# Values of an attention layer from seven products of halves, with output projections and a graph layer's values at other places

## The chip, the cores and the metric

The kernel runs on one core of one Trainium2 chip. The metric is device time in microseconds (us) of one execution. The core has TensorE (PE, matmuls; its weight loads are shown apart as PEld), VectorE (DVE), ScalarE (ACT), GpSimd (POOL) and SyncE (SP, which issues most DMAs here). [...]

## The reference, cut to what matters

Input is x (32, 512, 512) in float32: 32 batches of 512 nodes with 512 features. Two layers follow each other, each with a residual and a layer norm:

```python
x = _layernorm(x + _L0_gnn_ref(x, adj, W, a))     # graph attention: h = x @ W, softmax over e, alpha @ h
x = _layernorm(x + _L1_gnn_ref(x, adj, ...))      # 8 heads of 64, masked by adj

q, k, v = (split_heads(h @ W.T + b) for W, b in ((Wq, bq), (Wk, bk), (Wv, bv)))
scores = where(adj == 0, -inf, q @ k.T / 8)
out = softmax(scores) @ v                          # then out @ Wo.T + bo
```

The change concerns h @ Wv.T (the values, a 512x512x512 product per batch), and where out @ Wo.T and layer 0's alpha @ h stand in the order of work.

## The kernel before, in words

**Tiling.** Everything is float32. A batch is four tiles of 128 nodes. [...] Of the eight banks four (`ps_s`) are for attention scores; four (`ps_m`) go round for all else, the one that was given back first being taken first.

**Stretches.** The main loop takes, for each batch b, four pairs of heads (hp = 0 to 3). One turn is called a stretch here. In each stretch TensorE makes the scores of node tiles 0 and 1 (`head_scores`, ps, L593), then some other work (the first filler), then the scores of tiles 2 and 3, then probabilities times values of the pair before (`head_values`, pav, L628), then more other work (the second filler). The fillers are the rest of the model: layer 0 of the next batches (ph, po), the q and k projection of the next two pairs of heads (`project_two`, pw, L503), the values (`project_v`, pv, L575 calling L249) and the output projection of the batch before (`finish`, pf, L649).

**What the other engines do in a stretch.** VectorE subtracts the maximum from each of eight score tiles (L297), ScalarE takes the exponential (L602), VectorE transposes the eight results in blocks of 32 (L312) into a tile t, and takes the reciprocal of the row sums (tot, L611). SyncE then writes the sums out (d_tot, L613) and issues sixteen DMAs that move t into pt (L329), which `head_values` of the next stretch reads. There is one t, one pt and one tile for the inverted sums (inv, L616, two DMAs on POOL's queue), so each waits for the readers of the one before. After `head_values`, VectorE scales its result into ot (L636).

**Layer 0, one batch ahead.** In stretch hp 3, behind pt's sixteen issues, SyncE has three more DMAs in this order: d_most (512 single numbers to DRAM, L395), x of the next batch but one (1 MB, L145) and row (a read of d_most to all partitions, L400, which waits for the landing of d_most). In the next hp 0 stretch VectorE subtracts row from the scores (`l0_weights`, et, L429) and POOL adds h to x (`l0_add_h`, L355), when they have landed. In hp 1 `l0_values` (po, L437) follows, and the layer norm.

**Seven products.** `project_two` multiplies with seven products of half-sized blocks and sums of blocks instead of eight. The sums of weights are made once (`weight_sums`, L226), the sums of layer 1's input per batch (tx, `x1_sums`, L482 to L485, on POOL). A product is four matmuls of 256 columns; intermediate results are copied out by ScalarE (L527), one is added to another by POOL (p7, L555), and VectorE adds them to the last products (L539). The values use no such scheme: four tiles, each four matmuls of 512 columns and a copy on ScalarE (L576).

**What sets the order.** PE, DVE, ACT and SP keep the order in which the program calls the functions. POOL's order is chosen by a scheduler.

Of the kernel before, what the change touches and what calls it, by code (L numbers as in the profile page):

```python
# [14 lines left out]
P = 128  # L15
# [11 lines left out]
def kernel(  # L27
# [53 lines left out]
    PB = 9  # L81
# [34 lines left out]
    wqx_sb = const.tile([P, 3, 2, 2, P], F32, name="wqx_sb")  # L116
    wkx_sb = const.tile([P, 3, 2, 2, P], F32, name="wkx_sb")
    wv_sb = const.tile([P, FC, F], F32, name="wv_sb")
    wo_sb = const.tile([P, FC, F], F32, name="wo_sb")
    bq_sb = const.tile([P, FC], F32, name="bq_sb")  # L120
    bqs_sb = const.tile([P, FC], F32, name="bqs_sb")
# [21 lines left out]
    def load_x(b):  # L143
        x_sb = io.tile([P, NB, F], F32, name=f"x_{b}", tag="x", bufs=3)
        nc.sync.dma_start(x_sb, x[b].rearrange("(c p) f -> p c f", p=P))  # L145
        st["x1", b] = x_sb
# [79 lines left out]
    def weight_sums():  # L226

        for c in range(FC):  # L230
            nc.scalar.activation(wq_sb[:, c, :], wq_sb[:, c, :], AF.Identity, scale=SCALE)
        for w_t, x_t in ((wq_sb, wqx_sb), (wk_sb, wkx_sb)):
            v = w_t.rearrange("p c (s i d) -> p c s i d", s=2, i=2)
            lo, hi = slice(0, FC // 2), slice(FC // 2, FC)
            a11, a21 = v[:, lo, :, 0], v[:, lo, :, 1]
            a12, a22 = v[:, hi, :, 0], v[:, hi, :, 1]
            s1, s2, s4 = (x_t[:, i] for i in range(3))
            nc.vector.tensor_tensor(s1, a21, a22, ALU.add)
            nc.scalar.activation(a22, a22, AF.Identity, scale=-1.0)
            nc.vector.tensor_tensor(s2, s1, a11, ALU.subtract)  # L240
            yield
            nc.vector.tensor_tensor(s4, a12, s2, ALU.subtract)
            nc.vector.tensor_tensor(a21, a11, a21, ALU.subtract)
            yield

    def matmul_f(ps, lhs, rhs):

        for c in range(FC):
            nc.tensor.matmul(ps, lhs(c), rhs(c), start=(c == 0), stop=(c == FC - 1))  # L249

    def psum(name):
        return ps_m.tile([P, N], F32, name=name, tag="m")
# [139 lines left out]
    def l0_write(b):  # L392
        d = dram.tile([N], F32, name=f"d_most_{b}", tag="dmost")
        with nc.allow_non_contiguous_dma(reason="512 numbers"):
            nc.sync.dma_start(d.rearrange("(i p) -> p i", p=P), st["most", b])  # L395
        st["most", b] = d

    def l0_read(b):
        row = prob.tile([P, N], F32, name=f"row_{b}", tag="row", bufs=1)
        nc.sync.dma_start(row, st["most", b].partition_broadcast(P))  # L400
        st["row", b] = row
# [30 lines left out]
    def l0_values(b, i):  # L432
        h_sb, z = st["h", b], st["x1", b]
        et = st["et", b]
        po = ps_m.tile([P, F1 + 1], F32, name=f"po_{b}_{i}", tag="m")
        for j in range(NB):
            nc.tensor.matmul(  # L437
                po,
                et[:, j, i * P : (i + 1) * P],
                h_sb[:, j, 2:],  # L440
                start=(j == 0),
                stop=(j == NB - 1),
            )
        inv = small.tile([P, 1], F32, name=f"inv0_{b}_{i}", tag="inv0", bufs=2)
        nc.vector.reciprocal(inv, po[:, F1:])
        nc.vector.scalar_tensor_tensor(
            z[:, i, :F1], po[:, :F1], inv, z[:, i, :F1], ALU.mult, ALU.add
        )
# [119 lines left out]
        yield  # L568
        result(1, 0, b4, u2)

    def project_v(b, i):
        x1t = st["x1t", b]
        v = act.tile([P, F], F32, name=f"v_{b}_{i}", tag="v", bufs=6)
        ps = psum(f"pv_{b}_{i}")
        matmul_f(ps, lambda c: x1t[:, i, c, :], lambda c: wv_sb[:, c, :])  # L575
        nc.scalar.copy(v, ps)  # L576
        st["v", b, i] = v

    def head_scores(b, hp, i):
        qk = st["qk", b, hp]  # L580
# [41 lines left out]
    def head_values(b, hp, bank=None):  # L622
        pt, inv = st.pop(("pt", b, hp)), st.pop(("inv", b, hp))
        po = (bank or psum)(f"pav_{b}_{hp}")
        for c in range(NB):
            for j in range(2):
                head = 2 * hp + j
                nc.tensor.matmul(  # L628
                    po[j * D : (j + 1) * D, :],
                    st["v", b, c][:, head * D : (head + 1) * D],  # L630
                    pt[:, :, j, c, :, :].rearrange("p g i q -> p g (i q)"),
                    start=(c == 0),
                    stop=(c == NB - 1),
                )
        ot = act.tile([P, N], F32, name=f"ot_{b}_{hp}", tag="ot", bufs=6)
        nc.vector.tensor_tensor(  # L636
            ot.rearrange("p (g i q) -> p g i q", g=4, i=NB),
            po.rearrange("p (g i q) -> p g i q", g=4, i=NB),
            inv.rearrange("p (g q) i -> p g i q", g=4),
            ALU.mult,  # L640
        )
        st["ot", b, hp] = ot
# [37 lines left out]
    def steps(todo):  # L680
        for _ in todo:
            pass
# [18 lines left out]
        if i > 0:  # L701
            l0_norm(0, [i - 1])
    l0_norm(0, [NB - 1])
    steps(sums)
    masks1()
    l0_project(1, 0)
    l0_project(1, 1)
# [2 lines left out]
    l0_project(1, 3)  # L710
    l0_columns(1)
    x1_sums(0, nc.vector)
    project_v(0, 0)
    project_v(0, 1)
    steps(project_two(0, 0))
    l0_maxima(1)
    l0_write(1)
    l0_read(1)
    before = None
    for b in range(B):  # L720
        more = b < B - 1
        for hp in range(NP):

            head_scores(b, hp, 0)
            head_scores(b, hp, 1)
            if hp == 0:
                if more:
                    l0_scores(b + 1)  # L730
                if b > 1:
                    project_v(b, 0)
                if b > 0 and more:
                    project_v(b, 1)
            elif hp == 1:
                if more:
                    for i in range(NB):
                        l0_values(b + 1, i)
                        if i < NB - 1:
                            ln_stats(st["x1", b + 1], f"0_{b + 1}", i)  # L740
                else:
                    finish(b - 1, 0)
                if b + 2 < B:
                    load_xt(b + 2)
            elif hp == 2:
                if b > 0 and more:
                    finish(b - 1, 0)
                if b > 0 and more:
                    add_bias(b + 1)
            else:  # L750
                if b > 0:
                    if not more:
                        finish(b - 1, 3)
                    store(b - 1)
                if b + 2 < B:
                    for i in range(NB):
                        l0_project(b + 2, i)
                    l0_columns(b + 2)
                if b == 0:
                    project_v(1, 0)  # L760
            head_scores(b, hp, 2)
            head_scores(b, hp, 3)
            head_blocks(b, hp)
            if before is not None:
                head_values(*before)
            if hp == 3 and b + 2 < B:
                l0_maxima(b + 2)
                l0_write(b + 2)
                load_x(b + 2)
                l0_read(b + 2)  # L770
            if hp == 0:
                if not more:
                    project_v(b, 1)
                project_v(b, 2)
                project_v(b, 3)
                if more:
                    l0_weights(b + 1)
                    l0_add_h(b + 1)
            elif hp == 1:
                two = project_two(b, 1)  # L780
                if more:
                    ln_stats(st["x1", b + 1], f"0_{b + 1}", NB - 1)
                    ln_root(f"0_{b + 1}")
                if more:
                    l0_norm(b + 1)
                steps(two)
                if more:
                    x1_blocks(b + 1)
                    x1_sums(b + 1, nc.gpsimd)
            elif hp == 2:  # L790
                if b == 0:

                    pb = psum("pb")
                    matmul_f(
                        pb,
                        lambda c: bv_sb[:, c : c + 1].to_broadcast([P, P]),
                        lambda c: wo_sb[:, c, :],
                    )
                    nc.vector.tensor_tensor(bo_sb, pb, bo_sb, ALU.add)
                    add_bias(0)  # L800
                    add_bias(1)
                else:
                    finish(b - 1, 1)
                    finish(b - 1, 2)
                if b > 0 and more:
                    finish(b - 1, 3)
            elif more:
                steps(project_two(b + 1, 0))
            before = (b, hp)
    b = B - 1  # L810
# [64 lines left out]
```

## Time and profile before

| | |
|---|---|
| median of 3 runs | 3187.83 us (3183.2 to 3192.03) |
| the profiled execution | 3189.21 us, its span 3187.4 us |
| TensorE busy | 3131.1 us (98%) |
| VectorE, ScalarE, POOL busy | 2462.6, 1398.4, 772.8 us (77%, 44%, 24%) |
| SyncE's DMA queue | 434.23 MB, 56.9% of sixteen engines |
| mean granted TensorE clock | 0.994 |

The profile page counts busy time per engine, idle time with what ended it, and the chain of work that ended last. A float32 matmul stands as two instructions in it. The timeline gives start and length of merged instructions in us from the span's start, and in brackets the idle time before them and what ended it. In the text T0 is the start of a batch's hp 0 stretch on TensorE, T1 to T3 of the others.

### The profile page before, as it was taken

Reading aid. Unit: us, or ns where it says so; the run is one execution under the profiler, and the core shown is the slowest. Engines: PE = TensorE matmul, PEld = TensorE weight load, DVE = VectorE, ACT = ScalarE, POOL = GpSimd, SP = SyncE. Lnnn points to the kernel's source line nnn. Section 1 sums busy time; section 2 is a strip of 40 time slices with the busy share of each in tenths; the row PEclk is TensorE's granted clock in tenths of the full one; section 3 lists DMA queues with packets and bytes.
Section 4 is the critical chain, followed back from the end, with each engine's and each line's share of the span. In section 5 each row is a group of like instructions: output and inputs, shape, how many; then the busy total and the mean of one; then the engine's idle time right before and its main releaser. Section 6 shows DMA issues by size and latency. Waiting matters only on the chain.

```text
span 3187.4 us, 40275 instructions
## 1 busy us (share of the span) xinstructions
PE 3131.1 (98%) x11844; PEld 1769.4 (56%) x11844; DVE 2462.6 (77%) x5665; ACT 1398.4 (44%) x3057; POOL 772.8 (24%) x869
## 2 busy tenths in 40 slices
PE   7999999999999999999999999999999999999997
PEld 5555556555555555565565565555555555655543
DVE  4777777787778877787877787877788777878766
ACT  2444444444444444444444444444444444344432
POOL 1222221222222222312222222222223222222210
PEclk9999999999999999999999999999999999999999
DMA  5566566666666655665666565666666665656654
GB/s 155 126 156 149 148 146 159 138 148 154 153 141 155 154 146 148 148 160 143 149 159 148 144 156 142 151 151 154 144 153 152 151 147 139 162 136 152 137 136 116
DMA packets 259819, 470.64 MB, mean 148 GB/s; under 512 B 107472, under 2 KB 110032, under 8 KB 259600
## 3 DMA queue, kind: packets, MB, share of 16 engines
q1 hardware_dynamic: 247136, 434.23, 56.9%
q0 software_dynamic: 12464, 33.84, 4.1%
q8 instruction: 95, 1.56, 0.2%
q14 instruction: 124, 1.02, 0.1%
HBM read 132.65 MB, written 34.27 MB: 52 GB/s over the span
## 4 chain that ended last, share of the span: by engine, by line
PE 93%; DMA 3%; DVE 1%; issue 1%; SPq 1%; ACT 0%; DVEq 0%; ACTq 0%
PE pw L503 24%; PE ps L593 14%; PE pav L628 14%; PE pf L649 14%; PE pv L249 13%; PE po L437 7%; PE ph L249 7%; DMA d_most<-most 2%; SPq L329 1%; DMA pt<-t 0%; DMA row<-d_most 0%; DVE t L312 0%; DVE p L297 0%; DMA rows<-d_att 0%; DVE junk L297 0%
## 5 line engine op out<-in xcount | busy, mean ns | idle before, releaser
L602 ACT ACTIVATE p<-p,least 128x512 f32<-128x512 f32 x1024 | 725.5, 710 | 751.0 <-issue 402.4
L297 DVE CUSTOM_DVE_ANT_0 p<-ps,mask 128x512 f32<-128x512 f32 x1024 | 643.1, 684 | 296.4 <-PE ps L593 296.2
L312 DVE STREAM_TRANSPOSE t<-p 128x512 f32<-128x512 f32 x1024 | 622.4, 675 | 1.7 <-ACT p L602 1.5
L593 PE MATMUL ps<-qk 64*128 64x512 f32 x2048 | 513.5, 617 | 5.1 <-DVE least L297 4.9
L628 PE MATMUL pav<-pt,v 128*64 128x512 f32 x2048 | 469.8, 601 | 10.1 <-DMA pt<-t 4.4
L649 PE MATMUL pf<-wo_sb,ot 128*128 128x512 f32 x1024 | 459.7, 602 | 4.9 <-DVE ot L636 4.9
L249 PE MATMUL pv<-wv_sb,x1t 128*128 128x512 f32 x1024 | 456.6, 598 | 0.0
L616 POOL DMA_DIRECT2D inv<-d_tot x256 | 134.4, 528 | 1073.1 <-DVE least L297 560.0
L649 PEld LDWEIGHTS pf<-wo_sb,ot 128*128 128x128 f32 x1024 | 190.0, 191 | 271.8 <-issue 263.6
L249 PEld LDWEIGHTS pv<-wv_sb,x1t 128*128 128x128 f32 x1024 | 189.3, 190 | 263.7 <-issue 256.7
L593 PEld LDWEIGHTS ps<-qk 64*128 64x128 f32 x2048 | 178.5, 186 | 269.1 <-issue 187.8
L628 PEld LDWEIGHTS pav<-pt,v 128*64 128x64 f32 x2048 | 137.4, 137 | 327.8 <-issue 274.5
L437 PE MATMUL po<-h,et 128*128 128x257 f32 x1024 | 236.0, 389 | 6.8 <-ACT et L430 4.9
L249 PE MATMUL ph<-w_sb,xt 128*128 128x258 f32 x1024 | 235.8, 388 | 3.2 <-ACT x1t L468 2.9
L437 PEld LDWEIGHTS po<-h,et 128*128 128x128 f32 x1024 | 194.6, 193 | 59.2 <-ACT et L430 26.4
L249 PEld LDWEIGHTS ph<-w_sb,xt 128*128 128x128 f32 x1024 | 194.1, 192 | 54.9 <-DVE mv L263 22.0
L418 POOL TENSOR_TENSOR et<-et,mask0t 128x512 f32<-128x512 f32 x126 | 142.1, 1157 | 317.6 <-ACT et L414 317.6
L492 POOL TENSOR_TENSOR x<-x,bo_sb 128x512 f32<-128x512 f32 x128 | 158.4, 1271 | 190.6 <-DVE x1t_b L312 170.7
L602 ACT ACTIVATION_READ_ACCUMULATOR p<-p,least 128x1 f32 x1024 | 191.4, 187 | 0.0
L262 DVE BATCH_NORM_STATS2 stats<-x 128x6 f32<-128x512 f32 x256 | 177.6, 694 | 13.9
L576 ACT COPY v<-pv 128x512 f32<-128x512 f32 x128 | 71.2, 579 | 244.0 <-PE pv L249 244.0
L602 ACT ACT_TABLE_LOAD x63 | 80.8, 1283 | 215.3 <-DVE least L297 214.8
(103 smaller groups left out, 3683.3 us busy)
## 6 DMA issues: line engine op xcount, KB each, us to landing
pt<-t SPq DMA_DIRECT2D x2048, 128.0 KB, 3.5
x<-in_x_dram SPq DMA_DIRECT2D x32, 1024.0 KB, 14.2
inv<-d_tot POOLq DMA_DIRECT2D x256, 128.0 KB, 3.9
xt<-in_xt_dram SPq DMA_DIRECT2D x31, 1024.0 KB, 5.1
x1t<-x1t_b SPq DMA_DIRECT2D x496, 64.0 KB, 2.0
out_dram<-x SPq DMA_DIRECT2D x31, 1024.0 KB, 4.6
rows<-d_att SPq DMA_DIRECT2D x31, 512.0 KB, 3.9
row<-d_most SPq DMA_DIRECT2D x31, 256.0 KB, 5.7
```

The lines of the kernel that those rows point to most:

```text
L249: nc.tensor.matmul(ps, lhs(c), rhs(c), start=(c == 0), stop=(c == FC - 1))
L262: nc.vector.bn_stats(stats, z[:, i, :])
L297: nc.vector.tensor_tensor_reduce(out=out, in0=scores, in1=mask, scale=-1.0, scalar=MIN_INIT, op0=ALU.add, op1=ALU.min, accum_out=least,)
L312: nc.vector.transpose(t[:, :, :, i, :].rearrange("p r c q -> p c r q"), src.rearrange("p (c r k) -> p c r k", r=4, k=G),)
L418: engine.tensor_tensor(et[:, j, :], et[:, j, :], mask0t[:, j, :], ALU.add)
L437: nc.tensor.matmul(po, et[:, j, i * P : (i + 1) * P], h_sb[:, j, 2:], start=(j == 0), stop=(j == NB - 1),)
L492: nc.gpsimd.tensor_tensor(z[:, i, :], z[:, i, :], bo_sb, ALU.add)
L503: nc.tensor.matmul(ps[:, k * half : (k + 1) * half], weights(k, c), moving(c), start=start and k == 0 and c == 0, stop=c == FC // 2 - 1, s ...
L593: nc.tensor.matmul(ps, qk[rows, 0, i * P : (i + 1) * P], qk[rows, 1, :], start=True, stop=True)
L602: nc.scalar.activation(p, p, AF.Exp, bias=least, scale=-1.0, accum_out=total[:, j, i : i + 1])
L628: nc.tensor.matmul(po[j * D : (j + 1) * D, :], st["v", b, c][:, head * D : (head + 1) * D], pt[:, :, j, c, :, :].rearrange("p g i q -> p g ...
L649: nc.tensor.matmul(ps, st["ot", b, c][:, i * P : (i + 1) * P], wo_sb[:, c, :], start=(c == 0), stop=(c == FC - 1),)
```

## The change

1. `project_v(b)` makes a whole batch's values by seven products of halves (of Wv's columns and of node pairs). It is a generator with two pauses: the first product is made in front, then the pause; then four more products and the two second terms; then, after a pause, four additions on VectorE. ScalarE copies four intermediate tiles instead of four results, and POOL adds p7 and p5. The values stand in two tiles of two node tiles each, with two buffers instead of six.
2. In the hp 0 stretch the first product alone stands between the two groups of scores (before: two tiles of values), the rest behind `head_values`. The four additions stand behind `l0_weights` on VectorE. No values are made at the start of the kernel or in batch 0's hp 3 any more.
3. `l0_values` of the next batch moves, from batch 1 on, from between the scores of hp 1 to behind `head_values`, in front of pw. The load of xt moves behind it.
4. The output projections of tiles 0 to 3 of the batch before: tile 0 between the scores of hp 1, tile 1 between those of hp 2, tiles 2 and 3 at the end of hp 2. Before, tile 0 stood between the scores of hp 2 and the other three at its end.
5. `weight_sums` makes Wv's sums too, once at the start (three tiles more), behind the sums of x.

```diff
+    def project_v(b):
+        x1t, tx = st["x1t", b], st["tx", b]
+        half = F // 2
+        def product(ps, columns, weights, start=True):
+            for k in range(2):
+                for c in range(FC // 2):
+                    nc.tensor.matmul(
+                        ps[:, k * half : (k + 1) * half], columns(k, c), weights(c),
+                        start=start and k == 0 and c == 0,
+                        stop=c == FC // 2 - 1, skip_group_check=True,
+                    )
...
+        def result(i, j, ps, other):
+            nc.vector.tensor_tensor(
+                out[j][:, :, i * half : (i + 1) * half],
+                ps.rearrange("p (k d) -> p k d", k=2),
+                other.rearrange("p (k d) -> p k d", k=2),
+                ALU.add,
+            )
+        b1 = psum(f"pv1_{b}")
+        product(b1, b_(0, 0), a_(0, 0))
+        p1 = copy(b1, "p1")
+        yield
+        b3, b4 = psum(f"pv3_{b}"), psum(f"pv4_{b}")
+        product(b3, t_(0), s_(0))
+        p5 = copy(b3, "p5")
+        product(b4, t_(2), a_(1, 0))
+        p7 = copy(b4, "p7")
+        nc.gpsimd.tensor_tensor(p7, p7, p5, ALU.add)
+        product(b1, t_(1), s_(1), start=False)
+        u2 = copy(b1, "u2")
+        b2 = psum(f"pv2_{b}")
+        product(b2, b_(1, 0), a_(0, 1))
+        product(b3, b_(1, 1), s_(2), start=False)
+        product(b4, t_(3), a_(1, 1), start=False)
+        yield
+        result(1, 1, b1, p7)
+        result(0, 0, b2, p1)
+        result(0, 1, b3, u2)
+        result(1, 0, b4, u2)
...
             if hp == 0:
+                values = project_v(b)
+                next(values)
                 if more:
                     l0_scores(b + 1)
-                if b > 1:
-                    project_v(b, 0)
-                if b > 0 and more:
-                    project_v(b, 1)
             elif hp == 1:
-                if more:
-                    for i in range(NB):
-                        l0_values(b + 1, i)
-                        if i < NB - 1:
-                            ln_stats(st["x1", b + 1], f"0_{b + 1}", i)
+                if b == 0:
+                    l0_output(1)
                 else:
                     finish(b - 1, 0)
-                if b + 2 < B:
-                    load_xt(b + 2)
             elif hp == 2:
                 if b > 0 and more:
-                    finish(b - 1, 0)
-                if b > 0 and more:
+                    finish(b - 1, 1)
                     add_bias(b + 1)
...
             if hp == 0:
-                if not more:
-                    project_v(b, 1)
-                project_v(b, 2)
-                project_v(b, 3)
+                next(values)
                 if more:
                     l0_weights(b + 1)
                     l0_add_h(b + 1)
+                steps(values)
             elif hp == 1:
+                if b > 0 and more:
+                    l0_output(b + 1)
+                if b + 2 < B:
+                    load_xt(b + 2)
                 two = project_two(b, 1)
...
-                if b > 0 and more:
-                    finish(b - 1, 3)
+                elif more:
+                    finish(b - 1, 2)
+                    finish(b - 1, 3)
```

More of the change, by code (lines that the diff above doesn't have):

```diff
@@ L118 @@
     wv_sb = const.tile([P, FC, F], F32, name="wv_sb")
+    wvx_sb = const.tile([P, 3, 2, F // 2], F32, name="wvx_sb")
     wo_sb = const.tile([P, FC, F], F32, name="wo_sb")
@@ L231, in weight_sums @@
             nc.scalar.activation(wq_sb[:, c, :], wq_sb[:, c, :], AF.Identity, scale=SCALE)
-        for w_t, x_t in ((wq_sb, wqx_sb), (wk_sb, wkx_sb)):
-            v = w_t.rearrange("p c (s i d) -> p c s i d", s=2, i=2)
+        pairs = "p c (s i d) -> p i c s d"
+        for w_t, x_t, view, s in (
+            (wq_sb, wqx_sb, pairs, 2),
+            (wk_sb, wkx_sb, pairs, 2),
+            (wv_sb, wvx_sb, "p c (s i d) -> p i c (s d)", 1),
+        ):
+            v = w_t.rearrange(view, s=s, i=2)
             lo, hi = slice(0, FC // 2), slice(FC // 2, FC)
-            a11, a21 = v[:, lo, :, 0], v[:, lo, :, 1]
-            a12, a22 = v[:, hi, :, 0], v[:, hi, :, 1]
+            a11, a21 = v[:, 0, lo], v[:, 1, lo]
+            a12, a22 = v[:, 0, hi], v[:, 1, hi]
             s1, s2, s4 = (x_t[:, i] for i in range(3))
@@ L569, in project_two, with a_, s_, b_ @@
         result(1, 0, b4, u2)
[L571 to L577, printed above, removed]
+    def project_v(b):
[5 more added lines that the diff above has]
+                    nc.tensor.matmul(
+                        ps[:, k * half : (k + 1) * half],
+                        columns(k, c),
+                        weights(c),
+                        start=start and k == 0 and c == 0,
+                        stop=c == FC // 2 - 1,
+                        skip_group_check=True,
+                    )
+        def a_(i, f):
+            cols = slice(i * half, (i + 1) * half)
+            return lambda c: wv_sb[:, 2 * f + c, cols]
+        def s_(i):
+            return lambda c: wvx_sb[:, i, c, :]
+        def b_(f, j):
+            return lambda k, c: x1t[:, 2 * j + k, 2 * f + c, :]
+        def t_(i):
+            return lambda k, c: tx[:, i, k, c, :]
+        def copy(ps, name):
+            t = prob.tile([P, N], F32, name=f"{name}_{b}_v", tag="p", bufs=PB)
+            nc.scalar.copy(t, ps)
+            return t
+        out = []
+        for j in range(2):
+            v = act.tile([P, 2, F], F32, name=f"v_{b}_{j}", tag="v", bufs=2)
+            st["v", b, j] = v
+            out.append(v)
+        def result(i, j, ps, other):
[26 more added lines that the diff above has]
+        result(1, 0, b4, u2)
@@ L629, in head_values @@
                     po[j * D : (j + 1) * D, :],
-                    st["v", b, c][:, head * D : (head + 1) * D],
+                    st["v", b, c // 2][:, c % 2, head * D : (head + 1) * D],
                     pt[:, :, j, c, :, :].rearrange("p g i q -> p g (i q)"),
@@ L703 @@
     l0_norm(0, [NB - 1])
-    steps(sums)
+    next(sums)
+    next(sums)
     masks1()
@@ L712 @@
     x1_sums(0, nc.vector)
-    project_v(0, 0)
-    project_v(0, 1)
+    steps(sums)
     steps(project_two(0, 0))
@@ L718, with l0_output, output_bias @@
     l0_read(1)
+    def l0_output(b):
+        for i in range(NB):
+            l0_values(b, i)
+            ln_stats(st["x1", b], f"0_{b}", i)
+        ln_root(f"0_{b}")
+    def output_bias():
+        pb = psum("pb")
+        matmul_f(
+            pb, lambda c: bv_sb[:, c : c + 1].to_broadcast([P, P]), lambda c: wo_sb[:, c, :]
+        )
+        nc.vector.tensor_tensor(bo_sb, pb, bo_sb, ALU.add)
     before = None
@@ L758 @@
                     l0_columns(b + 2)
-                if b == 0:
-                    project_v(1, 0)
             head_scores(b, hp, 2)
@@ L765 @@
                 head_values(*before)
[L766 to L770, printed above, removed]
             if hp == 0:
-                if not more:
-                    project_v(b, 1)
-                project_v(b, 2)
-                project_v(b, 3)
+                next(values)
                 if more:
@@ L778 @@
                     l0_add_h(b + 1)
+                steps(values)
             elif hp == 1:
+                if b > 0 and more:
+                    l0_output(b + 1)
+                if b + 2 < B:
+                    load_xt(b + 2)
                 two = project_two(b, 1)
-                if more:
-                    ln_stats(st["x1", b + 1], f"0_{b + 1}", NB - 1)
-                    ln_root(f"0_{b + 1}")
                 if more:
@@ L791 @@
                 if b == 0:
[L793 to L799, printed above, removed]
+                    output_bias()
                     add_bias(0)
                     add_bias(1)
+                elif more:
+                    finish(b - 1, 2)
+                    finish(b - 1, 3)
                 else:
@@ L804 @@
                     finish(b - 1, 2)
-                if b > 0 and more:
-                    finish(b - 1, 3)
             elif more:
+                if b + 2 < B:
+                    l0_maxima(b + 2)
+                    l0_write(b + 2)
+                    load_x(b + 2)
+                    l0_read(b + 2)
                 steps(project_two(b + 1, 0))
```

## The prediction

> **What bounds the kernel now.** I read the page's busy times and chain first.
>
> ```profile
> span 3187.4 us, 40275 instructions
> PE 3131.1 (98%) x11844; PEld 1769.4 (56%) x11844; DVE 2462.6 (77%) x5665; ACT 1398.4 (44%) x3057; POOL 772.8 (24%) x869
> PE 93%; DMA 3%; DVE 1%; issue 1%; SPq 1%; ACT 0%; DVEq 0%; ACTq 0%
> ```
>
> TensorE is the bound. Next, the chain in order of time over one batch gives its pace:
>
> ```profile
> 1609.86 12.29 PE pw L503 x56
> 1622.15 1.92 PE ps L593 x8
> 1624.07 7.06 PE pv L249 x16
> 1631.13 1.92 PE ps L593 x8
> 1633.05 3.58 PE pav L628 x16
> 1636.63 7.06 PE pv L249 x16
> 1643.70 1.92 PE ps L593 x8
> ```
>
> No gap: hp 0 takes 21.55 us, the batch 96.81. The other stretches come from the same list: 26.84 (hp 1), 21.55 (hp 2), 26.9 (hp 3). So whatever TensorE saves counts, if nothing else arrives late. Hence the third view, the queues in order of time: SyncE first, then VectorE.
>
> ```profile
> 1612.91 0.36 SPq L613 DMA_DIRECT2D d_tot<-tot  x1
> 1613.45 11.18 SPq L329 DMA_DIRECT2D pt<-t  x16
> 1624.73 0.54 SPq L395 DMA_DIRECT2D d_most<-most  x1
> 1625.31 0.57 SPq L145 DMA_DIRECT2D x<-in_x_dram  x1
> 1634.96 0.33 SPq L400 DMA_DIRECT2D row<-d_most  x1
> 1639.68 0.36 SPq L613 DMA_DIRECT2D d_tot<-tot  x1
> ```
> ```profile
> 1642.16 3.42 DVE L429 TENSOR_TENSOR et<-et,row 128x512 f32<-128x512 f32 x4 [1.62 <-DMA row<-d_most]
> 1645.50 0.68 DVE L297 CUSTOM_DVE_ANT_0 p<-ps,mask 128x512 f32<-128x512 f32 x1
> ```
>
> Three late arrivals in hp 0: pt, row and x. Row made VectorE wait to T0+20, unseen by TensorE. And pt, in TensorE's own list and waits:
>
> ```profile
> 2603.12 5.35 PE L628 MATMUL pav<-pt,v 128*64 128x512 f32 x16 [1.94 <-DMA pt<-t]
> PE pav L628 <- DMA pt<-t: 4.4, 3, 1.9
> PE pav L628 <- DMA d_most<-most: 3.6, 3, 1.6
> POOL x L355 <- DMA x<-in_x_dram: 207.3, 31, 14.4
> ```
>
> The pav of hp 0 already waits at times; and 5.35 us against 3.58 means that the gap cost a further 1.7: the clock stood at 0.50 for the 3.4 us from 2604.5.
>
> [...] gaps of 1.94 and 2.04 were enough, while 1.52 to 1.86 and once 2.50 were not. [...] in 13 of 30 batches the last of hp 3's sixteen pt DMAs landed 5 to 12 us after its issue, while d_most's 512 four-byte writes were under way; without them (last two batches) it took 2.6 to 3.0. [...] inv's DMAs stand on POOL behind the addition to x, which waited 207 us in all.
>
> **The change, part by part.**
>
> Products: pv's two groups are 7.06 + 7.06 = 14.12 us a batch. Seven products of four 256-column matmuls are as many as pw has; pw takes 12.29. Gain 1.83 us, times 31 = 56.7. Batch 0 gains more, since 7.0 us of values leave the start and fill what were gaps of 2.5 and 3.0: about 5.0. Together 61.7. The 0.44 us a matmul of pw includes the extra weight loads.
>
> VectorE gets four additions at 0.69 (pf's row, also a PSUM and an SBUF operand) = 2.8 us a batch, ScalarE nothing (four copies for four), POOL one addition at 1.31. Wv's sums: four operations on VectorE (0.69 x3 + 1.13) and one on ScalarE, 3.8 us once, beside 12.3 us of pw: nothing; at most 3.8 if pw's own additions waited for them.
>
> Moves: po and pf cost TensorE the same elsewhere. New stretches: hp 0 1.92 + 1.76 + 1.92 + 3.58 + 10.53 = 19.7; hp 1 26.84 + 3.5 = 30.4; hp 2 18.05; hp 3 as before. In hp 1 VectorE has po's division and statistics (4 x 1.6) after ot, then the root and the norm. From T1+16 that gives po done at 22.4, norm done at 26.3, and pw's fourth product needs po's last bank at 23.4 (free at 21.5), its additions the norm's end by 28.6. It fits; about 0.2 us is lost as po's fourth tile waits for ot's bank. xt's load then goes out behind hp 1's pt, around T1+26, and is needed at T1+50: nothing. Hp 2's pav comes 14.4 us after the reciprocal of its sums instead of 17.9; pt there needs 13.6 (median; 14.9 at most): nothing, at most 0.5 in a few batches.
>
> Now what loses its cover.
>
> (a) pav of hp 0 reads hp 3's pt. It stood 20.13 us after tot; now 20.13 - (7.06 - 1.76) = 14.83, and hp 3 itself is unchanged. Landings, 13 to 14.75 us after tot in 17 batches, are in time; in 13 they were 15.9, 16.8, 18.5, 21.5, 21.6, 20.2, 16.1, 15.9, 18.9, 17.4, 22.1, 19.5, 21.6. Beyond 14.83 that sums to 53 us.
>
> (b) pf of tile 0 now stands at T0 + 19.65 + 1.92 = T0+21.6 and takes the bank that is given back first, that of the first product, by VectorE's first addition. This one reads p7. In the order of the changed program POOL's p7 stands (batches 1 to 30) behind l0_add_h and behind inv's two DMAs. Batch 16: x landed at T0+18.6, the adds took 3.05, inv 1.04, then p7 1.3: T0+24.0; addition and latency 0.8: pf starts 3.2 late. In general x's landing minus 15.3. VectorE's other condition is row: landing + 3.2 (et) + 0.8, i.e. landing minus 17.6. Over the batches x landed at T0+15.0 to 18.8 (median 16.6), row at 16.0 to 20.4.
>
> (c) hp 0's own pt: sums are ready at T0+13.5 (ScalarE: four exponentials to 4.8, p1's copy, layer 0's scores 4.5, four more to 12.6; VectorE's last transpose behind it); its landing 13.5 later is T0+27.0, just when pav wants it. 0.2 us a batch, hidden by (b).
>
> (a) and (b) overlap: when pt is late, TensorE comes later to pf. So I took the larger per batch: 2.0 to 7.3 where pt was late, 0.3 to 3.5 elsewhere. That sums to 90 us over 30 batches. Of these, 21 are 1.9 us or longer; a half clock after each would add 36, none 0; with 14 of them 24.
>
> Behind a waiting pav stand pv's rest and all scores of hp 1; behind a waiting pf the scores of tiles 2 and 3. VectorE, queued behind the first addition, does not delay them further: the maxima of hp 1 come 2 us after pf's new start, and pf lasts 3.5.
>
> Sum, against the profiled execution: its span 3187.4, less its own five pav stalls in batches 1 to 30 (1.52, 1.52, 0.47, 1.94, 1.62) and the half clock, 8.8 = 3178.6; less 61.7; plus 90; plus 24 = 3231. The execution adds 1.8 to its span and lay 1.4 above the median: 3231.
>
> **Rivals.**
>
> Cover holds: if pt, x and row land as in the better batches, (a) and (b) vanish, and the gain stays whole: 3187.8 - 61.7 = 3126. Against it: p7's place in POOL's queue is fixed, and x is issued behind the same DMAs. The total ends on the faster side when stalls stay below 1.9 us a batch, 59 in all; that needs x at T0+16 and at most six late pt. For it: [...] batches 6 to 19 had none. Single-sided relief is worth 3160 to 3175. 0.22.
>
> Only POOL's order bites, pt is rarely late: stalls by (b) alone sum to 55, half clocks to 17: 3178.6 - 61.7 + 72 = 3189, no change. The three times of before speak against it: 3183 to 3192 over a floor of 3180 without pav stalls means that very late pt landings come in every run. 0.12.
>
> VectorE becomes the bound: it is busy 24.5 of hp 1's 26.9 us now, and gets 1.6 more (pf's addition and statistics) on top of starting 5 us late. If each operation there ran 5% longer, po's banks come late and each batch loses about 1 us more: 3262. 0.13.
>
> Forecast: 0.53, own range 3200 to 3258.
>
> **How the numbers follow.** No change is within 0.3%, 9.6 us: about what a measurement can tell here. Of the forecast's 0.53 I count 0.48 slower, 0.04 same, 0.01 faster; rival one 0.20 faster, 0.02 same; rival two 0.04 slower, 0.05 same, 0.03 faster; rival three 0.13 slower. Slower 0.65, same 0.11, faster 0.24. The range leaves out the whole gain and the far end of rival three: 3165 to 3258.
>
> **What would show it.** Right: pv 12.3 us a batch in TensorE's list; pav in hp 0 waiting for pt or d_most, 4 us and more in a third of the batches; pf waiting for VectorE in most others, 0.3 to 3.5 us, VectorE's v addition waiting for POOL's p7 or x; more half-clock slices; hp 2 without gaps. Wrong: p7's end before T0+20, hp 3's pt within 14.8 us of tot throughout, or waits on po's banks in hp 1.

## The result, and the profile after

The changed kernel takes 3215.76 us (median of 6 runs, 3198.34 to 3240.61), the kernel before 3182.23 us (6 runs, 3178.76 to 3192.03) beside it: ratio 1.0106, 95% interval 1.0064 to 1.0148. It is slower by 1%. The profiled execution took 3217.2 us.

The page of the changed kernel, same parts as shown of before:

```profile
span 3215.2 us, 42167 instructions
PE 3099.6 (96%) x12612; PEld 1922.6 (60%) x12612; DVE 2556.7 (80%) x5797; ACT 1413.4 (44%) x3058; POOL 816.3 (25%) x901
PE 80%; DMA 9%; DVE 5%; SPq 2%; issue 1%; ACT 1%; DVEq 0%; ACTq 0%
```

TensorE is busy for 31.5 us less, and yet the span is 27.8 us longer: its share of the chain fell from 93% to 80%, and DMA and VectorE took what it gave up. Its list of waits says where:

```profile
PE pf L718 <- DVE v L619: 26.4, 17, 2.7
PE pav L697 <- ACT p L671: 19.7, 6, 5.5
PE pav L697 <- DMA pt<-t: 12.6, 5, 4.9
...
```

Columns: total us, number, longest. The waits at pf are the forecast's (b), a bank that is given back late. At pav several releasers are named (ScalarE's et and d_most stand further down with 11.1 and 7.2 us), but in hp 0 the cause is one: in the eleven batches where its pav waited, it started 0.1 to 0.5 us after the landing of the last of hp 3's sixteen pt DMAs, in all others 0.8 us or more after it. ScalarE's exponentials and et, which pav doesn't read, merely ended just before it. That is (a), hp 3's pt landing late. In TensorE's timeline, (a) in batch 5 (T0 = 547.2), then (b) in batch 17 (T0 = 1728.7):

```profile
558.51 5.51 PE L697 MATMUL pav<-pt,v 128*64 128x512 f32 x16 [5.50 <-ACT p L671]
...
1748.64 1.99 PE L662 MATMUL ps<-qk 64*128 64x512 f32 x8
1752.38 3.70 PE L718 MATMUL pf<-wo_sb,ot 128*128 128x512 f32 x8 [1.76 <-DVE v L619]
```

pav took 5.51 us behind its gap, against 3.65 in batches without one: the clock records show 0.50 for 6.83 us from 555.5. Why pf waited 1.76 us in batch 17 stands on VectorE, POOL and SyncE, in this order:

```profile
1746.94 4.79 DVE L435 TENSOR_TENSOR et<-et,row 128x512 f32<-128x512 f32 x4 [3.74 <-DMA row<-d_most]
1751.65 1.28 DVE L619 TENSOR_TENSOR v<-pv,p_v 128x512 f32<-128x512 f32 x2
```
```profile
1745.22 3.05 POOL L361 TENSOR_TENSOR x<-x,h 128x256 f32<-128x256 f32 x4 [5.37 <-DMA pt<-t]
...
1749.29 1.28 POOL L635 TENSOR_TENSOR p_v<-p_v 128x512 f32<-128x512 f32 x1
```
```profile
1731.49 0.53 SPq L401 DMA_DIRECT2D d_most<-most  x1
...
1740.56 0.33 SPq L406 DMA_DIRECT2D row<-d_most  x1
```

SyncE could issue row only 9.1 us after d_most, whose landing it waits for. x let POOL start at T0+16.5 (it landed 0.1 us before; pt, which the line names, is not read there). Row let VectorE start at T0+18.2, and the first v addition freed pf's bank at T0+23.6. The subtraction took 4.79 us, not the 3.2 of the forecast.

### The profile page after: what moved, and what is told of

Same layout as the page of the kernel before. It is cut to its first block, busy times and chain, and to the rows that moved or that the text cites. A ratio compares the mean times of both kernels' runs of the same rounds, so it can differ in the third digit from the quotient of the medians.

```text
span 3215.2 us, 42167 instructions
## 1 busy us (share of the span) xinstructions
PE 3099.6 (96%) x12612; PEld 1922.6 (60%) x12612; DVE 2556.7 (80%) x5797; ACT 1413.4 (44%) x3058; POOL 816.3 (25%) x901
## 4 chain that ended last, share of the span: by engine, by line
PE 80%; DMA 9%; DVE 5%; SPq 2%; issue 1%; ACT 1%; DVEq 0%; ACTq 0%
PE pw L509 24%; PE pf L718 13%; PE pav L697 13%; PE ps L662 11%; PE po L443 7%; PE ph L255 7%; DMA d_most<-most 5%; PE pv L585 5%; DMA row<-d_most 3%; DVE et L435 2%; SPq L335 1%; DVE p L303 1%; DMA pt<-t 1%; ACT et L420 1%; DVE t L318 0%
## 5 line engine op out<-in xcount | busy, mean ns | idle before, releaser
L318 DVE STREAM_TRANSPOSE t<-p 128x512 f32<-128x512 f32 x1024 | 632.8, 678 | 36.8 <-ACT p L671 18.9
L697 PE MATMUL pav<-pt,v 128*64 128x512 f32 x2048 | 486.4, 618 | 52.6 <-ACT p L671 19.7
L718 PE MATMUL pf<-wo_sb,ot 128*128 128x512 f32 x1024 | 469.9, 607 | 28.6 <-DVE v L619 26.4
L697 PEld LDWEIGHTS pav<-pt,v 128*64 128x64 f32 x2048 | 144.4, 141 | 380.9 <-issue 268.0
L435 DVE TENSOR_TENSOR et<-et,row 128x512 f32<-128x512 f32 x124 | 140.9, 1194 | 72.2 <-DMA row<-d_most 72.2
L533 ACT COPY p<-pw 128x512 f32<-128x512 f32 x192 | 108.9, 584 | 179.8 <-PE pw L509 176.3
L274 ACT ACTIVATE rstd<-mv,eps 128x4 f32<-128x4 f32 (+1 forms) x70 | 20.7, 297 | 322.2 <-DVE mv L269 317.8
## 6 DMA issues: line engine op xcount, KB each, us to landing
x<-in_x_dram SPq DMA_DIRECT2D x32, 1024.0 KB, 13.2
```

Source lines behind the costliest of these rows:

```text
L318: nc.vector.transpose(t[:, :, :, i, :].rearrange("p r c q -> p c r q"), src.rearrange("p (c r k) -> p c r k", r=4, k=G),)
L435: nc.vector.tensor_tensor(et[:, j, :], et[:, j, :], row, ALU.subtract)
L697: nc.tensor.matmul(po[j * D : (j + 1) * D, :], st["v", b, c // 2][:, c % 2, head * D : (head + 1) * D], pt[:, :, j, c, :, :].rearrange("p ...
L718: nc.tensor.matmul(ps, st["ot", b, c][:, i * P : (i + 1) * P], wo_sb[:, c, :], start=(c == 0), stop=(c == FC - 1),)
```

## The experiments

The theory to be tested: the scattered write of d_most (512 writes of 4 bytes) holds up the landing of pt, x and row, and the change took the cover that hid it, which is TensorE's other work between the issue of a transfer and its reader. The rivals: (1) the order in POOL's and VectorE's queues does it, whatever the write is; (2) the moves of po and pf do it; (3) VectorE or TensorE has become slower in itself.

**1. The write itself.** The numbers are transposed on VectorE and leave in 16 runs of 128 bytes. For that they stand in one tile padded to 32 columns (before: two buffers of four). Nothing else changes, in the changed kernel and in the kernel before:

```diff
-        with nc.allow_non_contiguous_dma(reason="512 numbers"):
-            nc.sync.dma_start(d.rearrange("(i p) -> p i", p=P), st["most", b])
+        turned = small.tile([P, G], F32, name=f"turned_{b}", tag="turned", bufs=1)
+        nc.vector.transpose(turned, most_sb)
+        runs = d.rearrange("(i g k) -> g i k", i=NB, g=4)
+        for g in range(4):
+            nc.sync.dma_start(runs[g], turned[g * G : g * G + NB])
...
```

> The changed kernel, with one thing else: the 512 numbers of d_most leave the chip as 16 runs of 128 bytes (a 32 x 32 transpose on VectorE, then four DMAs of four partitions each) instead of 512 writes of 4 bytes. My theory (the scattered writes hold up the landing of hp 3's last pt, and with it of row, so that TensorE waits at hp 0's pav and at output tile 0): both waits go, some 45 us at pav and 26 us at pf, and with them some 25 us of half clock; 3216 - 96 = 3120, and up to 3150 if x still lands at T0+15 and p7 with it. Rival 1 (the places in the queues do it: p7 stands on POOL behind x's addition and inv, whatever the writes are): pav's waits shrink, pf's stay, 3160 to 3190. Rival 2 (VectorE or TensorE's own work under the new order is what costs): 3200 or more, with small waits in the trace and longer stretches of work.

> The kernel before, with d_most written as 16 runs of 128 bytes as in the other run. It says what the writes cost where the cover of 7 us still stands. My theory: only the few pav waits of before and their half clock go, some 9 us: 3170 to 3178. If the writes cost more than stands in TensorE's waits (a rival: they slow all DMA, or VectorE, all the time), it gains 20 us and more. If the transpose and three more DMAs cost as much as they save, 3180 to 3190.

Measured: the changed kernel 3133.53 us, ratio to before 0.9850 (0.9837 to 0.9863); the kernel before 3178.78 us, ratio 0.9987 (0.9978 to 0.9995). One edit is worth 82 us in one kernel and 3.5 us in the other. The changed kernel with few writes, SyncE and then POOL in its batch 17 (T0 = 1687.0), and TensorE's longest wait at pav:

```profile
1688.95 1.45 SPq L406 DMA_DIRECT2D d_most<-turned  x4
...
1691.64 0.35 SPq L411 DMA_DIRECT2D row<-d_most  x1
```
```profile
1698.18 2.62 POOL L363 TENSOR_TENSOR x<-x,h 128x256 f32<-128x256 f32 x4
```
```profile
PE pav L702 <- DMA pt<-t: 8.3, 5, 4.5
```

Row goes out 2.7 us behind d_most instead of 9.1; x's addition starts at T0+11.2, without waiting. p7 stands behind x's addition and inv as before, and ends at T0+18 to 20. No wait at pf for v is left in the list, and most batches take 95.25 us without a gap. VectorE is busy for 80% of the span here too, so it is not the bound, and POOL's order alone costs nothing. The moves are still there. So none of the three rivals explains the whole loss; what the moves cost comes under 4.

**2. Is it the write's presence, its queue or its number of pieces?** To the version with few writes a spare write of the same 512 numbers is added, into memory that nobody reads: in SyncE's queue as 512 pieces (the line shown); the same from ScalarE's queue (`nc.scalar`); and in SyncE's as 128 pieces of 16 bytes (`"(p i) -> p i"`).

```diff
+            nc.sync.dma_start(spare.rearrange("(i p) -> p i", p=P), st["most", b])
```

> The version with d_most in 16 runs of 128 bytes (3133), with a spare write of 512 numbers of 4 bytes added in front of it, into memory that nobody reads. Row no longer reads what the scattered write brings, so only its presence in the queues is left. My theory (the small writes hold up what else is landing, whoever waits): pav's waits for hp 3's pt come back, and row and x land late again with pf's waits: 3195 to 3225. Rival (the scattered write is only slow itself, so that row came late; pt's lateness has another cause): 3133 to 3150, without waits at pav.

> As the run with the spare scattered write, but issued by ScalarE into its own queue, while pt, x and row stay in SyncE's. If the place behind the scattered write in one queue is what delays them: 3133 to 3150. My theory [...]: nearly as slow as the spare write in SyncE's queue, 3190 to 3225, with waits at pav for hp 3's pt.

> As the run with the spare scattered write in SyncE's queue (3223), but the same 512 numbers go out as 128 pieces of 16 bytes (the four of a partition side by side) instead of 512 pieces of 4. If the number of pieces sets how long the others' landing is held up (my theory): about a quarter of the 90 us comes back, 3140 to 3165, with the pav waits nearly gone. If any write of small pieces does it, whatever their number: 3200 and more.

Measured: 3223.08 us (ratio 1.0121, 1.0095 to 1.0146), 3262.75 us (1.0238, 1.0201 to 1.0275), 3134.75 us (0.9841, 0.9822 to 0.9860). A write that nobody waits for brings the whole loss back. SyncE with the spare write in its own queue, and TensorE's wait at pf:

```profile
1742.09 1.42 SPq L409 DMA_DIRECT2D d_most<-turned  x4
...
1751.10 0.35 SPq L414 DMA_DIRECT2D row<-d_most  x1
```
```profile
PE pf L726 <- DVE v L627: 37.6, 20, 4.0
```

The contiguous d_most behind the spare write takes 9.0 us to let row go here (4.9 to 10.2 in batches 1 to 30; 2.4 to 3.6 without the spare write). The gaps at hp 0's pav are back too, 31.4 us in nine batches. In ScalarE's queue the write goes out as soon as the maxima are ready, in the middle of pt's issues, and SyncE's sixteen issues themselves took 16 us (median of hp 3; 10.5 without it):

```profile
1757.63 16.04 SPq L337 DMA_DIRECT2D pt<-t  x16
```
```profile
PE pav L705 <- DMA d_most<-turned: 55.1, 21, 4.4
PE pw L517 <- ACT p L541: 27.9, 29, 2.1
```

pav in hp 0 waited in 29 of 30 batches. So the queue is not what holds them: this write stood in ScalarE's queue, pt's DMAs in SyncE's, and pav's idle time came to 85.8 us. What holds pt there, no run shows. I had expected 3190 to 3225; what I missed are the 27.9 us at pw, where ScalarE's copies stood behind the DMA instruction (at 1760.84 and 1761.25 in the batch shown), and that pt meets the write every time. With 128 pieces the cost is gone altogether (a quarter was expected). Whether the number of pieces or their size decides is not separated: both changed. One DMA that stands in all versions says something on it: d_tot is 256 pieces of 16 bytes, and it lands 2.0 us after its issue, d_most 10.2 us (medians of the kernel before). Half the number in a fifth of the time is not one price for every piece.

The packet records of the changed kernel show more of how the write does it. All of its pieces had passed 2.2 us after its issue, and then the sixteen DMA engines moved little until d_most had landed: in batch 17 34 GB/s from 1733.5 to 1741.5, and 304 in the four us after that. With few writes they moved 286 GB/s from 1691.0 to 1695.5. And in the eleven batches where pt was late, the last of its packets of 4096 bytes had passed 2.5 to 7.4 us before the landing was reported; in the other nineteen 0.3 to 1.2 us. So pt's numbers were not late on their way, the report of their landing was. Why they moved so little, and why the report is held in eleven batches only, no run shows.

**3. The cover given back.** Three more of the first products stand in front of hp 0's pav; the scattered write stays. POOL's scheduler then puts p7 in front of x's addition, so the run changes two things: pav's waits test the cover, and a change at pf could come from either.

```diff
-        b2 = psum(f"pv2_{b}")
-        product(b2, b_(1, 0), a_(0, 1))
+        yield
         product(b3, b_(1, 1), s_(2), start=False)
         product(b4, t_(3), a_(1, 1), start=False)
+        b2 = psum(f"pv2_{b}")
+        product(b2, b_(1, 0), a_(0, 1))
...
             head_blocks(b, hp)
+            if hp == 0:
+                next(values)
```

> The changed kernel, with the third, fourth and second stretch of the first products (5.3 us of TensorE) moved in front of hp 0's pav, so that pav stands again 20 us behind hp 3's sums, as in the kernel before; the scattered writes stay. In this order POOL's p7 comes in front of the addition to x. My theory: the pav waits fall from 45 us to under 15 and the half clocks with them, pf waits stay where row is late (about half of 26 us), so 3216 - 30 - 15 - 10 = about 3160, range 3145 to 3180. Rival 1 (pf's wait on VectorE is the larger cause, pav's only moves on): 3190 to 3210, with pf's waits grown by what pav's lost. Rival 2 (VectorE or TensorE's work itself): 3205 and more.

Measured 3170.33 us (ratio 0.9971, 0.9960 to 0.9982), inside the range expected. hp 3's pt still landed up to 21.9 us after its sums, but pav stood 20.37 us behind them: its median slack (from the landing to its start) rose from 1.2 to 6.6 us, and it waited in one batch, not in eleven. pf's waits fell to 4.7 us. New waits of 0.4 to 2.2 us came at hp 1's pav, for hp 0's own pt, in 22 of 30 batches; these 21 us are the larger part of the 37 us by which it stays behind the version with few writes.

**4. The two halves of the change.** The moves alone (old values, new places of po, pf and xt's load), and the products alone (old places), each with the scattered write and with few writes.

```diff
             elif hp == 1:
-                if b == 0:
-                    l0_output(1)
-                else:
-                    finish(b - 1, 0)
+                if more:
+                    for i in range(NB):
+                        l0_values(b + 1, i)
...
             elif hp == 2:
                 if b > 0 and more:
-                    finish(b - 1, 1)
+                    finish(b - 1, 0)
...
```

(The products alone, against the changed kernel; the moves alone are the reverse, made in the kernel before. The maxima and x's load, which two of the expectations name among the moves, are called at the same place of the order in both kernels; only their lines stand elsewhere.)

> The kernel before with the moves of the change alone (layer 0's values in front of pw, output projections spread, maxima and x's load of the next batch behind hp 3's filler), values still four products of whole tiles in their old places. My theory (the loss comes from the cover that the values' products gave in hp 0, not from the moves): within 10 us of before, 3175 to 3195. Rival 2 (VectorE is late in hp 1 because po and the norm stand closer together, or the moved loads are late): 3205 to 3230, about as slow as the whole change.

> The kernel before with the seven products alone: po stands again in hp 1's first filler, three tiles of pf in hp 2, the maxima and x's load of the next batch in front of hp 3's filler. My theory (cover in hp 0 is what decides): hp 3's pt has the same 14.8 us as in the changed kernel, so its pav waits stay at about 45 us with their half clock; po now stands where pf stood, and needs et's exponentials, which follow row's subtraction (done at T0+20.8 in the changed kernel) by 2.2 us and more, where TensorE comes at T0+21.6: waits of 1.5 to 4 us in every batch, against 26 us at pf. 3225 to 3270. Rival (the loss comes from the moves, as the run of the moves alone at 3248 suggests: it lost 2 us a batch at hp 1's pav): with po's 7.1 us in front of it this pav does not wait, and the products' gain comes through, 3140 to 3175.

> The moves alone (values as four products of whole tiles), with d_most as 16 runs of 128 bytes. My theory: the 2 us a batch that the moves alone cost are hp 0's own pt, 13.2 us after its sums at hp 1's pav, which now stands 3.5 us earlier; that pt does not run beside the scattered writes, so they stay: 3225 to 3245. Rival (these waits too come from the scattered writes): 3172 to 3190.

> The products alone (old places of po, pf and the loads), with d_most as 16 runs of 128 bytes. My theory: without the scattered writes hp 3's pt is there after 14 us and row's subtraction ends at T0+16.4 as in the changed kernel with few writes, so et's exponentials are done before TensorE comes to po at T0+21.6: 3125 to 3145, as fast as the whole change with few writes. Rival (po in hp 1's first filler needs the move, whatever the writes are): waits at po in every batch, 3160 to 3190.

| median us, ratio to before (interval) | scattered write | few writes |
|---|---|---|
| neither | 3182.23 | 3178.78, 0.9987 (0.9978 to 0.9995) |
| moves alone | 3248.41, 1.0212 (1.0198 to 1.0226) | 3252.22, 1.0219 (1.0202 to 1.0237) |
| products alone | 3217.51, 1.0107 (1.0085 to 1.0128) | 3124.79, 0.9814 (0.9799 to 0.9828) |
| both (the change) | 3215.76, 1.0106 (1.0064 to 1.0148) | 3133.53, 0.9850 (0.9837 to 0.9863) |

My expectation for the moves alone was wrong by 60 us. Hp 1 of the kernel before, then of the moves alone, on TensorE, and the latter's waits:

```profile
1645.54 7.21 PE L437 MATMUL po<-h,et 128*128 128x257 f32 x32
...
1654.60 3.65 PE L628 MATMUL pav<-pt,v 128*64 128x512 f32 x16
```
```profile
1774.00 3.70 PE L649 MATMUL pf<-wo_sb,ot 128*128 128x512 f32 x8
...
1781.33 3.65 PE L628 MATMUL pav<-pt,v 128*64 128x512 f32 x16 [1.71 <-DMA pt<-t]
```
```profile
PE pav L628 <- DMA pt<-t: 60.8, 29, 4.7
```

A single pf tile (3.5 us) stands where po (7.1) stood, so hp 1's pav comes 3.5 us sooner, and hp 0's pt had only 1.5 us of slack (median). The other 2 us are waited for in 29 of 30 batches. This pt does not run beside the scattered write, hence few writes change nothing (3252). In the whole change the products give that time back: the stretch between the two groups of scores shrinks from 7.06 to 1.92 us, so hp 0's sums come sooner (T0+13.6 instead of 17.5, medians), and 3.5 us of pv more stand behind hp 0's pav. So the halves do not add up: +66 and +35 alone make +34 together.

The products alone lose as much as the whole change while the write is scattered: pav waits as in the change, and po waits for et's exponentials, as expected:

```profile
PE po L443 <- ACT et L436: 28.5, 18, 4.1
```

With few writes they are the fastest kernel of all, 3124.79 us, 1.9% below before; a full batch takes 95.23 us without a gap. The moves then cost 9 us more; in the traces some 5 us of that are pav waits in batches 1, 15, 16 and 30.

**5. Which gate holds pf's bank?** Either VectorE's v additions go in front of row's subtraction (then p7 alone is left), or p7 is added on VectorE (then row alone is left).

```diff
                 next(values)
+                steps(values)
                 if more:
                     l0_weights(b + 1)
                     l0_add_h(b + 1)
-                steps(values)
```
```diff
-        nc.gpsimd.tensor_tensor(p7, p7, p5, ALU.add)
+        nc.vector.tensor_tensor(p7, p7, p5, ALU.add)
```

> The changed kernel, with VectorE's four v additions in front of the subtraction of row from et; POOL keeps its order (x's addition, inv, p7). Output tile 0's bank then hangs on p7 alone. In the changed kernel's profile the subtraction ended last in 16 of 31 batches and p7 in 15. My theory: pf's waits fall from 26 us to 10 to 18, pav's 45 us stay, 3195 to 3210. If row is the only gate: pf's waits go to under 5, 3180 to 3195. If p7 is the only gate: no change, 3212 to 3220.

> The changed kernel, with the addition to p7 on VectorE instead of POOL; it stands in front of the subtraction of row from et, so p7 no longer waits for x's addition and inv. Output tile 0's bank then hangs on row's subtraction alone. My theory (both gates bind, about half of the batches each): pf's waits fall from 26 us to 10 to 18, pav's stay, 3195 to 3210. If p7 was the only gate: pf's waits under 5, 3180 to 3195. If row was: no change, 3212 to 3220.

Measured: 3225.51 us (1.0143, 1.0118 to 1.0168) and 3203.37 us (3188.7 to 3221.63; 1.0073, 1.0044 to 1.0101); neither interval is clear of the change's own. Waits of TensorE, first with the additions in front, then with p7 on VectorE:

```profile
PE ps L662 <- DVE least L303: 17.4, 18, 2.0
PE pf L718 <- DVE v L619: 5.3, 7, 1.6
```
```profile
PE pf L718 <- DVE v L619: 9.2, 9, 2.3
```

Each gate alone leaves 5 to 9 of the 26 us, less than I had expected. (The profiled execution of the second kernel was the fastest of its six, so its 9.2 is from a good one.) In the first kernel nothing was won: the subtraction now stands in front of hp 1's maxima, whose late end made the scores wait 17.4 us instead of 3.0. The wait moved to the next in VectorE's queue. And the two gates make each other worse. The subtraction in the changed kernel, with the additions in front (POOL then idle beside it), and with p7 on VectorE (only x's addition and inv beside it); the columns after the count are busy us and mean ns of one:

```profile
L435 DVE TENSOR_TENSOR et<-et,row 128x512 f32<-128x512 f32 x124 | 140.9, 1194 | 72.2 <-DMA row<-d_most 72.2
```
```profile
L435 DVE TENSOR_TENSOR et<-et,row 128x512 f32<-128x512 f32 x124 | 77.0, 682 | 0.0
```
```profile
L435 DVE TENSOR_TENSOR et<-et,row 128x512 f32<-128x512 f32 x124 | 97.3, 843 | 63.4 <-DMA row<-d_most 58.2 <-POOL x L361 5.0
```

In batch 17 the subtraction overlaps x's addition, inv and p7, and it ended at 1751.73, 1.2 us after p7. On average it took 682 ns without POOL's work beside it and 1194 ns with it; which additions or issues held VectorE, and how, no run here shows.

## Why the prediction was right, and where its sum was off

The side, the mechanism (readers that lose their cover) and both places were right, and the time lay 0.5% below the forecast. The terms, by the profiled spans (before 3187.4; before with few writes 3175.5; changed with few writes 3132.0; changed 3215.2):

- **Products.** Forecast 61.7. Measured 43.5 (3175.5 - 3132.0), or 50.2 with the products alone (3125.3); the difference is what the moves cost beside them. Mis-sized was "1.83 a batch": a full batch fell from 96.81 to 95.24, 1.57. pv takes 1.92 + 10.63 = 12.55 us and not pw's 12.29, since it stands in two stretches, and the first product of each lasts 1.92 and 1.84 instead of 1.73. It also counted 31 batches; only 28 showed the full gain. The 5.0 for the start was right: 4.8 (start 6.2 and batch 0 0.4 shorter, batch 1 1.8 longer).
- **(a) hp 3's pt.** Forecast 13 late landings and 53 us. In the trace 11 of 30 came later than 14.83 us after the sums, at most 20.4 (before: 22.1); the gaps at hp 0's pav sum to 35.9 us.
- **(b) pf's bank.** Right in both conditions; their sizes were off in both directions. x landed at T0+13.2 to 17.5 and row at 14.1 to 19.2, both ranges one to two us sooner than before (d_most landed 8.1 to 10.9 us after its issue, against 8.3 to 13.4), and p7 ended at T0+18.7 to 22.9. But the subtraction took 4.9 us (median, 5.7 at most) instead of 3.2. That POOL's work beside it prolongs VectorE's subtraction (682 ns a tile alone, 1194 in the changed kernel) was missing. pf waited 26.4 us in 17 batches.
- **(c) hp 0's own pt.** 0.2 us a batch, hidden, holds for the whole change: with few writes hp 1's pav waits in three batches, 1.8 us in all. That it would be 2 us without the products, I did not see before the run of the moves alone. Hp 2's pt, put at nothing or 0.5 us in a few batches, was waited for 1.0 to 1.3 us in batches 6, 9 and 12.
- **The sum of stalls.** Forecast 90. Measured in batches 1 to 30 72.0 us of gaps, 7.8 of which the version with few writes has too: 64.2. Half clock: forecast 24, an estimate from a few gaps of before; records of 88.3 us against 39.3 with few writes, half of the difference lost at clock 0.50: 24.5. The forecast had 14 slices of half clock, the trace has ten spells, five of them twice as long: that this term fits is partly luck. Together 88.7; the two spans differ by 83.2.
- **Balance.** Gain 18 too large, stalls with half clock 25 too large; the floor 3.1 too high (3178.6 against 3175.5), and 5.5 of the measured stalls not seen in the spans: 25 - 18 + 3 + 6 makes the 16 us between 3231 and 3215. Errors of opposite effect made the total look better than its terms.
- **The rivals.** "Cover holds" at 3126 is what the kernel does once the write is gone (3125 to 3134): its price was right, its condition wasn't met. "Only POOL's order" falls with pav's waits, and POOL's order costs nothing without the write. "VectorE becomes the bound" falls: it is 80% busy in the versions without stalls too, and no wait of hp 1 at po's banks was seen.

"Moves: po and pf cost TensorE the same elsewhere" is true of their durations, and says nothing of what they covered.

## What to carry to other kernels

Where TensorE saves time, ask of each transfer that it reads how long before it was issued, and subtract what the edit takes out of that window; an edit that costs nothing in instructions can cost 2 us a batch in cover (the moves alone), and two such edits can cancel in part (66 and 35 us alone, 34 together). Here a small DMA of 512 separate numbers cost 90 us through what landed beside it, though nobody waited for it: make such a write contiguous first, then shorten the cover. When a wait is taken away by reordering an engine's queue, look at what comes next in it: here the maxima, for which the scores waited 17.4 us.

## What the runs showed of the hardware

- A write of 512 pieces of 4 bytes, 2 KB in all, landed 8.1 to 10.9 us after its issue in the changed kernel. Row could follow a contiguous write (16 runs of 128 bytes) after 2.4 to 3.6 us, and after 4.9 to 10.2 with a write of 512 pieces in front of it. Such a spare write cost 90 us over 31 batches, one of 128 pieces of 16 bytes 1 us.
- While it was landing, the sixteen DMA engines moved 34 GB/s for 8 us (batch 17), and 304 in the four us after it. Landings of pt were reported up to 7.4 us after the last packet had passed.
- Issued from ScalarE's queue in the middle of sixteen pt DMAs, it stretched SyncE's issue of these from 10.5 to 16 us.
- A VectorE subtraction of two tiles in SBUF (128x512, float32) took 682 ns on average with GpSimd idle, 843 ns with x's addition and inv's issue beside it, and 1194 ns with p7's addition too.
